# Turning half of each later image's x on VectorE instead of TensorE in a two-layer attention kernel

## The chip, the cores and the metric

The kernel runs on one core of a Trainium2 chip. The metric is the device time of one execution in microseconds. All data is fp32. The engines are named as in the profile: PE (TensorE), PEld (its weight loads), DVE (VectorE), ACT (ScalarE), POOL (GpSimd), SP (SyncE, which here only issues transfers).

## The reference

Input x has 8 images of 32x32 tokens with 512 channels. Two layers follow one another. The change lies in the first:

```
x_flat = x.reshape(8, 1024, 512)
# group norm: 32 groups of 16 channels, over all tokens of an image
mu, var = mean and variance over (tokens, the 16 channels of a group)
x_norm = (x - mu) * rsqrt(var + 1e-6) * gn_scale + gn_bias
q, k, v = split(x_norm @ w_qkv + b_qkv, 3)          # 8 heads of 64
out = softmax(q k^T / 64 per head) @ v               # 1024 queries, 1024 keys
x = x_flat + out @ w_out + b_out
```

(1/64 is the product of the two scalings of q and of k by 1/sqrt(64).) The second layer takes a layer norm of that result, a projection, a 7x7 depthwise convolution of stride 2, from which sampling points come, bilinear samples as keys and values, an attention of 1024 queries over 256 keys, an output projection, and an MLP with residual. Of it only the convolution matters here, since a large part of it is computed during the first layer.

## The kernel before, in words

The first pass handles layer 0. For each image it needs x with the channels on the partitions: xT, two blocks of [128, 4, 512] (partition, chunk c, token), where channel = c*128 + partition. Tokens come in 8 tiles of 128 (`x`, two buffers). `load_x` fetches a tile with 128 partitions of 2 KB, issued by POOL. `turn(t)` transposes it with four PE transposes (moving operand the identity, weights the 128x128 piece of x), copies the PSUM tile to xT by ACT, and issues the load of the tile two later. `two_tiles(i)` runs four bn_stats of 256 tokens on DVE; `gather`, `means`, `deviations`, `factors` make the group statistics with a small matrix `gmat` that averages over the partitions of a group, and `norm(blk)` scales xT in place (ACT for images after the first).

The main loop goes over images b (called blocks here, 0 to 7), four head pairs and 8 query tiles: 32 units per block, 256 in all. The step `att.push` of a unit issues:

1. scores: 16 matmuls into two PSUM tiles `sc` (one for each head of the pair, two buffers in all, so the next unit writes the same two);
2. on DVE the maximum `nmax` of each, on ACT the exponential `e` of each;
3. everything that is due before unit + 0.8 (`before`);
4. on DVE two transposes `sq` of 128x1024; after each second unit 16 transfers by SP turn `sq` into `et`, which the `av` matmuls of two to four units later read;
5. everything that is due before unit + 1 (`after`).

All other work is put on places in units by hand: `at(place, step)`, and `run_due` issues what is due in order of place. A place 8.4 is thus in unit 8 after its scores and exponentials, and 8.9 is after its DVE transposes. `InOrder` keeps every engine's instructions in this program order, and each engine works through its own queue strictly in it. The places that the prediction names:

- `norm_steps` for the next image: turns of tiles 0 to 7 at 8.4, 8.45, 16.4, 16.45, 22.4, 22.45, 23.4, 23.45; statistics at 9.85, 17.86, 22.86, 23.95; the group statistics at 23.97 to 25.81, the scaling at 25.85 and 26.85. Image 0 has the same list before the loop.
- `qkv_steps`, `value_steps`: one projection of 16 or 32 matmuls in most units.
- `out_steps` (blocks 1 to 7, for the image before): `fetch` and `add` (POOL, tile `xr`), `out` (PE), `summed` (DVE: `xr`, `stats`, `mv`, then a power on POOL), `norm` (DVE `hat`, then two products of 128x512 on POOL); `norm` of the rows stands at 4.85, 6.85, 7.85, 8.85, 12.85, 14.85, 15.85, 16.85.
- `conv_chunk` (blocks 2 to 7 in units 1 to 24, blocks 1 to 7 from unit 26): the 49 taps of 128 channels. Most are made by ACT (`part_x`, two buffers, named `oa` for the first) and added to `oa` by POOL; the rest by DVE (`od`). In a unit half of ACT's taps stand at .05 and on, the other half at .9 and on, DVE's at .86 and on. So the late taps of a unit lie in ACT's queue ahead of the next unit's exponentials.

The steps that the change touches:

Of the kernel before, what the change touches and what calls it, by code (L numbers as in the profile page):

```python
# [9 lines left out]
F32 = mybir.dt.float32  # L10
I32 = mybir.dt.int32
AF = mybir.ActivationFunctionType
ALU = mybir.AluOpType
AX = mybir.AxisListType
# [3 lines left out]
P = 128  # L18
# [3 lines left out]
C = 512  # L22
NC = C // P
NT = S // P
QB = 512
NQB = S // QB
NQT = QB // P
# [3 lines left out]
GRP = 16  # L31
# [3 lines left out]
SQ = 32  # L35
NSQ = P // SQ
# [205 lines left out]
def attention_then_deformable_attention(  # L242
# [30 lines left out]
    nc = tc.nc  # L273
    x_tok = x.rearrange("b h w c -> b (h w) c")
# [8 lines left out]
    ident = const.tile([P, P], F32, tag="ident", name="ident")  # L283
# [7 lines left out]
    def mm_tile():  # L291
        return ps_mm.tile([P, QB], F32, tag="mm", name="mm")

    def by_chunk(w):
        return w.rearrange("(c p) o -> p c o", p=P)
# [6 lines left out]
    def load_cols(pool, v, name):  # L302
        t = pool.tile([P, v.shape[0] // P], F32, tag=name, name=name)
        with nc.allow_non_contiguous_dma(reason="a vector onto partitions"):
            nc.sync.dma_start(t, v.rearrange("(c p) -> p c", p=P))
        return t

    def load_row(pool, v, name):
        t = pool.tile([P, C], F32, tag=name, name=name)
        nc.sync.dma_start(t, v.partition_broadcast(P))  # L310
        return t
# [32 lines left out]
    def rstd(dst, var, eps):  # L344
        nc.vector.tensor_scalar(dst, var, eps, None, ALU.add)
        nc.gpsimd.tensor_tensor(dst, dst, minus_half[:, 0 : dst.shape[1]], ALU.pow)
# [15 lines left out]
    def at(place, step):  # L362
        due.append((place, len(due), step))
# [37 lines left out]
    with ExitStack() as l0:  # L401
        wp = l0.enter_context(tc.tile_pool(name="w0", bufs=1))
        work = l0.enter_context(tc.tile_pool(name="work0", bufs=2))

        nc = InOrder(tc)
        NX = 2
        NX_T = 3
        xs = {}

        def load_x(b, t):  # L410
            if b < B:
                xs[b, t] = work.tile([P, C], F32, tag="x", name="x", bufs=NX)
                nc.gpsimd.dma_start(xs[b, t], x_tok[b][ts(t, P), :])


        x2 = work.tile([P, NC, QB], F32, tag="xT", name="x2", bufs=NX_T)
# [3 lines left out]
            xs[0, NQT + t] = x2[:, t, :]  # L420
            nc.sync.dma_start(xs[0, NQT + t], x_tok[0][ts(NQT + t, P), :])
        wqkv = wp.tile([P, NC, 3 * C], F32, tag="wqkv", name="wqkv")
        gsc = load_cols(wp, gn_scale, "gsc")
        gbi = load_cols(wp, gn_bias, "gbi")
        bqkv = load_cols(wp, b_qkv, "bqkv")
        for i in (1, 0, 2):
            nc.sync.dma_start(wqkv[:, :, ts(i, C)], by_chunk(w_qkv)[:, :, ts(i, C)])
        bout = load_row(wp, b_out, "bout")
        room_w = {}

        def load_weight(w):
# [7 lines left out]

        gmat = wp.tile([P, P], F32, tag="gmat", name="gmat")  # L440
        nc.gpsimd.memset(gmat, 1.0 / GRP)
        g3 = gmat.rearrange("p (g c) -> p g c", c=GRP)
        ng = P // GRP
        nc.gpsimd.affine_select(
            out=g3, in_=g3, pattern=[[-GRP, ng], [0, GRP]], compare_op=ALU.is_ge,
            fill=0.0, base=0, channel_multiplier=1,
        )
        nc.gpsimd.affine_select(
            out=g3, in_=g3, pattern=[[GRP, ng], [0, GRP]], compare_op=ALU.is_ge,
            fill=0.0, base=GRP - 1, channel_multiplier=-1,  # L450
        )
        att = MovedAttention(nc, ident, ps_mm, ps_sc, ps_av, work, dram, 1)
        xTs, qkv, vals = {}, {}, {}

        def norm_steps(b, start, places):

            room = {}

            def turn(t):
                blk, i = divmod(t, NQT)  # L460
                if i == 0:
                    xTs[b, blk] = work.tile([P, NC, QB], F32, tag="xT", name="xT", bufs=NX_T)
                if t == 0:
                    room["stats"] = work.tile([P, NC, NT // 2, 6], F32, tag="stats", name="stats", bufs=1)
                ps = mm_tile()
                for c in range(NC):
                    nc.tensor.transpose(ps[:, ts(c, P)], xs[b, t][:, ts(c, P)], ident)
                nc.scalar.copy(xTs[b, blk][:, :, ts(i, P)], ps.rearrange("p (c q) -> p c q", q=P))
                if b > 0:
                    load_x(b + (t + NX) // NT, (t + NX) % NT)  # L470
                elif t < NX:
                    load_x(1, t)

            def two_tiles(i):
                blk, half = divmod(i, NQT // 2)
                for c in range(NC):
                    nc.vector.bn_stats(
                        room["stats"][:, c, i, :], xTs[b, blk][:, c, ts(half, 2 * P)]
                    )


            def gather():
                mv = room["mv"] = work.tile([P, NC, 2], F32, tag="mv", name="mv")
                stats = room["stats"]
                for c in range(NC):
                    nc.vector.bn_aggr(mv[:, c, :], stats[:, c, :, :].rearrange("p s f -> p (s f)"))

            def means():
                mv = room["mv"]
                ps = mm_tile()  # L490
                for m in range(2):
                    half = ds(m * HD, HD)
                    nc.tensor.matmul(
                        ps[half, 0:NC], lhsT=gmat[:, half], rhs=mv[:, :, 0], start=True, stop=True
                    )
                mu = room["mu"] = work.tile([P, NC], F32, tag="mu", name="mu")
                nc.vector.tensor_copy(mu, ps[:, 0:NC])
                dev = room["dev"] = work.tile([P, NC], F32, tag="dev", name="dev")
                nc.vector.tensor_tensor(dev, mv[:, :, 0], mu, ALU.subtract)
                nc.vector.tensor_tensor(dev, dev, dev, ALU.mult)  # L500
                nc.vector.tensor_tensor(dev, dev, mv[:, :, 1], ALU.add)

            def deviations():
                ps = mm_tile()
                for m in range(2):
                    half = ds(m * HD, HD)
                    nc.tensor.matmul(
                        ps[half, 0:NC], lhsT=gmat[:, half], rhs=room["dev"], start=True, stop=True
                    )
                room["rs"] = work.tile([P, NC], F32, tag="rs", name="rs")  # L510
                rstd(room["rs"], ps[:, 0:NC], 1e-6)

            def factors():
                nc.vector.tensor_tensor(room["rs"], room["rs"], gsc, ALU.mult)
                room["add"] = work.tile([P, NC], F32, tag="nadd", name="nadd")
                nc.vector.tensor_tensor(room["add"], room["mu"], room["rs"], ALU.mult)
                nc.vector.tensor_tensor(room["add"], gbi, room["add"], ALU.subtract)

            def norm(blk):
                xT, add, rs = xTs[b, blk], room["add"], room["rs"]  # L520
                for c in range(NC):
                    if b == 0:
                        nc.vector.tensor_scalar(
                            xT[:, c, :], xT[:, c, :], rs[:, c : c + 1], add[:, c : c + 1],
                            ALU.mult, ALU.add,
                        )
                    else:
                        nc.scalar.activation(
                            xT[:, c, :], xT[:, c, :], AF.Identity,
                            bias=add[:, c : c + 1], scale=rs[:, c : c + 1],  # L530
                        )

            steps = [
                *(lambda t=t: turn(t) for t in range(NT)),
                *(lambda i=i: two_tiles(i) for i in range(NT // 2)),
                gather, means, deviations, factors,
                *(lambda blk=blk: norm(blk) for blk in range(NQB)),
            ]
            for place, what in zip(places, steps):
                at(start + place, what)  # L540
# [150 lines left out]
        def conv_chunk(b, cb, n):  # L691
# [79 lines left out]
        first_values = (1.3, 2.3, 3.3, 4.3)  # L771
        value_places = [(-1.7, 2.3, 3.6, 4.3), (10.3, 18.3, 19.3, 20.3)]
        norm_places = [
            *(8.4, 8.45, 16.4, 16.45, 22.4, 22.45, 23.4, 23.45),
            *(9.85, 17.86, 22.86, 23.95),
            *(23.97, 24.03, 25.03, 25.81, 25.85, 26.85),
        ]
        out_places = [3.3, 5.3, 6.3, 7.3, 11.3, 13.3, 14.3, 15.3]
# [10 lines left out]
        for b in range(B):  # L789
# [22 lines left out]
            for hp in range(NHP):  # L812
                for qt in range(NT):
                    n = first + hp * NT + qt
                    if n % per == 0 and b > 0:
# [6 lines left out]
                    t = qkv[b, hp]  # L822
# [5 lines left out]
                        q=t["q", qt // NQT][:, ts(qt % NQT, P)],  # L828
# [8 lines left out]
    with ExitStack() as l1:  # L837
        nc = tc.nc


        def pool(name, bufs=1):
            return l1.enter_context(tc.tile_pool(name=name, bufs=bufs, reuse_waits="tile"))

        first, raw, late, late2, cv, cvhat, wp = (
            pool(n) for n in ("first", "raw", "late", "late2", "cv", "cvhat", "w2")
        )
        work = pool("work1", 2)
        nc = InOrder(tc)
# [89 lines left out]
        chat, room = {}, {}  # L938
# [385 lines left out]
```

## Time and profile before

| what | value |
|---|---|
| median of 3 runs | 3404.53 us (3399.92 to 3406.07) |
| the profiled execution's own time | 3397.38 us |
| its span, first to last instruction | 3395.7 us |
| granted PE clock, mean | 0.99 |
| PE, DVE, ACT, POOL busy | 97%, 73%, 53%, 46% |
| first pass (scores of unit 0 to the last of its work) | 35.8 to 2042 us |
| turns `mm<-ident,x` on PE | 256 instructions, 37.0 us busy |
| `xT<-mm` copies on ACT | 64, mean 588 ns |
| `x<-in_x_dram` issues on POOL | 60, mean 558 ns |

A row of a group gives line, engine, operation, output<-inputs, shape and count, then busy time and mean duration of one in ns, then the engine's idle time just before it and who ended it. A row of a timeline gives start and duration in us, the engine, the operation, how many in a row, and in brackets the idle time before with its releaser. Nearly all instructions are recorded under line 54, the helper that issues them, so rows are told apart by their tiles.

### The profile page before, as it was taken

How to read it: one execution, taken by the hardware profiler on the slowest of the kernel's cores; microseconds unless marked ns; L12 is line 12 of the kernel's file. 1: busy time of each engine (PE TensorE's matmuls, PEld its weight loads, DVE VectorE, ACT ScalarE, POOL GpSimd, SP SyncE). 2: the span in 40 equal slices, each digit the busy share in tenths (PEclk: the TensorE clock that was granted, in tenths of full speed). 3: DMA queues.
4: the chain of work that ended last, by engine and by line, in shares of the span. 5: the costliest groups of instructions: out<-in, count | busy, mean ns of one | idle time of the engine just before them, and what ended most of it. 6: DMA issues, size and time to landing. Idle time of an engine off the chain costs nothing. (4 is left out here: it accounts for less than half of the span.)

```text
span 3395.7 us, 59693 instructions
## 1 busy us (share of the span) xinstructions
PE 3298.7 (97%) x21736; PEld 1348.9 (40%) x21736; DVE 2480.5 (73%) x3373; ACT 1811.4 (53%) x3927; POOL 1547.6 (46%) x1903
## 2 busy tenths in 40 slices
PE   7999999999999999999999998889999999999998
PEld 3344444444344444344344343433333333333332
DVE  5776788888888888888898885157767586664654
ACT  3443365576576566566567561245565555554442
POOL 1002226656746746755755763215455354631322
PEclk9999999999999999999999999899999999999999
DMA  5666766766766766776767667446566565665653
GB/s 153 177 179 164 210 179 196 215 176 183 228 181 184 218 187 180 210 202 179 216 185 187 202 191 205 138 159 200 185 203 197 183 203 185 208 214 191 215 177 126
DMA packets 446645, 642.57 MB, mean 189 GB/s; under 512 B 77104, under 2 KB 240944, under 8 KB 444304
## 3 DMA queue, kind: packets, MB, share of 16 engines
q1 hardware_dynamic: 415712, 536.67, 54.5%
q0 software_dynamic: 29488, 100.00, 9.6%
q8 instruction: 172, 2.82, 0.3%
q10 hardware_dynamic: 1152, 2.10, 0.2%
q14 instruction: 121, 0.99, 0.1%
HBM read 246.38 MB, written 123.73 MB: 109 GB/s over the span
## 5 line engine op out<-in xcount | busy, mean ns | idle before, releaser
L54 ACT ACTIVATE e<-sc,nmax 128x1024 f32<-128x1024 f32 (+1 forms) x1024 | 803.4, 798 | 490.7 <-DVE nmax L54 487.9
L54 DVE TENSOR_REDUCE nmax<-sc 128x1 f32<-128x1024 f32 (+1 forms) x640 | 751.7, 1215 | 337.0 <-PE sc L54 333.0
L54 POOL TENSOR_TENSOR oa<-part_x,oa 128x256 f32<-128x256 f32 x852 | 640.7, 752 | 552.6 <-ACT part_x L54 506.3
L54 DVE STREAM_TRANSPOSE sq<-e 128x1024 f32<-128x1024 f32 x640 | 766.2, 1228 | 156.6 <-ACT e L54 125.1
L54 ACT ACTIVATE part_x<-pad_x,dww_x 128x256 f32<-128x256 f32 x852 | 442.3, 547 | 251.8 <-POOL oa L54 250.7
L54 PE MATMUL sc<-k,q 64*64 64x512 f32 x4096 | 516.6, 602 | 13.5 <-ACT e L54 10.3
L54 PE MATMUL av<-et,v 128*64 128x256 f32 x4096 | 502.5, 388 | 14.1 <-DMA et<-sq 12.5
L54 PE MATMUL mm<-xT,wqkv 128*64 128x512 f32 x2048 | 463.1, 594 | 3.2 <-issue 3.2
L54 PEld LDWEIGHTS av<-et,v 128*64 128x64 f32 x4096 | 275.4, 137 | 332.0 <-issue 170.3
L54 POOL TENSOR_TENSOR chunk<-parts,chunk 128x256 f32<-128x256 f32 x240 | 186.8, 778 | 277.3 <-ACT parts L54 263.4
L54 POOL TENSOR_TENSOR mv<-mv,minus_half 128x1 f32<-128x1 f32 x128 | 76.5, 598 | 510.3 <-DVE mv L54 509.8
L54 PEld LDWEIGHTS sc<-k,q 64*64 64x64 f32 x4096 | 139.2, 132 | 322.1 <-issue 204.0
L54 PEld LDWEIGHTS mm<-xT,wqkv 128*64 128x64 f32 x2048 | 148.3, 138 | 255.0 <-issue 239.6
L54 DVE SCALAR_TENSOR_TENSOR od<-pad_x,dww_x,od 128x256 f32<-128x256 f32 x276 | 232.2, 841 | 5.5
L54 PE MATMUL mm<-wo,attH 128*64 128x512 f32 x1024 | 234.8, 598 | 0.7 <-DVE attH L54 0.7
L54 PE MATMUL mm<-w,attT 128*64 128x512 f32 x1024 | 231.5, 596 | 2.0 <-DVE attT L54 2.0
L54 PE MATMUL mm<-wqkv,xT 128*64 128x256 f32 x2048 | 232.1, 379 | 0.0
L54 PE MATMUL mm<-wm,zT 128*64 128x512 f32 x1024 | 230.7, 592 | 1.0 <-ACT zT L54 1.0
L54 PE MATMUL mm<-hat_h,wqq 128*64 128x512 f32 x1024 | 230.8, 593 | 0.0
L54 ACT ACTIVATION_READ_ACCUMULATOR e<-sc,nmax 128x1 f32 x1024 | 209.3, 204 | 0.0
L54 ACT ACTIVATE parts<-pad,dww 128x256 f32<-128x256 f32 x240 | 126.4, 552 | 124.8 <-POOL chunk L54 124.4
L54 PEld LDWEIGHTS mm<-wqkv,xT 128*64 128x64 f32 x2048 | 148.1, 137 | 77.6 <-issue 6.4
(164 smaller groups left out, 3390.9 us busy)
## 6 DMA issues: line engine op xcount, KB each, us to landing
et<-sq SPq DMA_DIRECT2D x2048, 128.0 KB
sq_d<-sq SPq DMA_DIRECT2D x128, 512.0 KB
et<-sq_d SPq DMA_DIRECT2D x128, 512.0 KB
inv<-rs_d SPq DMA_DIRECT2D x256, 128.0 KB
hat_h<-hat_d SPq DMA_DIRECT2D x16, 1024.0 KB
xr<-mid SPq DMA_DIRECT2D x64, 256.0 KB
x<-in_x_dram POOLq DMA_DIRECT2D x60, 256.0 KB
out_dram<-res POOLq DMA_DIRECT2D x60, 256.0 KB
```

What stands on the lines that cost most here:

```text
L54: return self.tc.keep_in_program_order(op(*args, **kwargs))
```

## The change

Channels are laid out in fours per partition: channel = partition*4 + c. The weights wqkv and the vectors gsc and gbi are loaded accordingly, a group of 16 channels now lies on 4 partitions, so `gmat` has blocks of 4, and the sums over the four columns of a group are made by two small reductions, with one value per partition for mean and deviation.

For images after the first, tiles 0 to 3 are loaded by four transfers, one for each quarter of the channels: quarter r goes to partitions 32r to 32r+31, partition 32r+q holding that quarter (128 channels, 512 bytes) of the tokens 4q to 4q+3. One DVE transpose in blocks of 32x32, which reads and writes with a step of 4 elements, then makes the tile of xT directly in SBUF. Tiles 4 to 7, and all of image 0, are turned by PE as before, but read x with a step of 4 elements. The loads leave `turn` and become steps `more(t)` of their own. New places: turns at 1.9, 4.9, 7.9, 10.9 for tiles 0 to 3; loads at 4.2 (tile 2), 7.2 (tile 3), 10.2 and 12.5 (tiles 4, 5), 22.46 and 22.47 (tiles 6, 7), 26.4 and 27.2 (tiles 0 and 1 of the image after); the second statistics step at 15.86 instead of 17.86.

```diff
@@ load_x
-                nc.gpsimd.dma_start(xs[b, t], x_tok[b][ts(t, P), :])
+                src, dst = x_tok[b][ts(t, P), :], xs[b, t]
+                if b > 0 and t < NQT:
+                    src = src.rearrange("(q t) (r x) -> r q t x", t=NSQ, r=NSQ)
+                    dst = dst.rearrange("p (t x) -> p t x", t=NSQ)
+                    for r in range(NSQ):
+                        nc.gpsimd.dma_start(dst[ts(r, SQ)], src[r])
+                    return
+                nc.gpsimd.dma_start(dst, src)
...
-        gsc = load_cols(wp, gn_scale, "gsc")
-        gbi = load_cols(wp, gn_bias, "gbi")
+        gsc, gbi = (wp.tile([P, NC], F32, tag=n, name=n) for n in ("gsc", "gbi"))
+        for tile_, v in ((gsc, gn_scale), (gbi, gn_bias)):
+            nc.sync.dma_start(tile_, v.rearrange("(p c) -> p c", p=P))
...
-            nc.sync.dma_start(wqkv[:, :, ts(i, C)], by_chunk(w_qkv)[:, :, ts(i, C)])
+            nc.sync.dma_start(
+                wqkv[:, :, ts(i, C)], w_qkv.rearrange("(p c) o -> p c o", p=P)[:, :, ts(i, C)]
+            )
...
@@ turn
-                ps = mm_tile()
-                for c in range(NC):
-                    nc.tensor.transpose(ps[:, ts(c, P)], xs[b, t][:, ts(c, P)], ident)
-                nc.scalar.copy(xTs[b, blk][:, :, ts(i, P)], ps.rearrange("p (c q) -> p c q", q=P))
+                to = xTs[b, blk][:, :, ts(i, P)]
+                if b > 0 and blk == 0:
+                    nc.vector.transpose(
+                        to.rearrange("p c (q t) -> p t c q", t=NSQ),
+                        xs[b, t].rearrange("p (t i c) -> p t c i", t=NSQ, i=SQ),
+                    )
+                else:
+                    ps = mm_tile()
+                    by_row = xs[b, t].rearrange("p (i c) -> p c i", c=NC)
+                    for c in range(NC):
+                        nc.tensor.transpose(ps[:, ts(c, P)], by_row[:, c], ident)
+                    nc.scalar.copy(to, ps.rearrange("p (c q) -> p c q", q=P))
+                if b == 0 and t < NX:
+                    load_x(1, t)
+
+            def more(t):
                 if b > 0:
                     load_x(b + (t + NX) // NT, (t + NX) % NT)
-                elif t < NX:
-                    load_x(1, t)
...
@@ means, deviations, factors
-                nc.vector.tensor_copy(mu, ps[:, 0:NC])
+                nc.vector.tensor_reduce(mu, ps[:, 0:NC], AX.X, ALU.add)
...
-                rstd(room["rs"], ps[:, 0:NC], 1e-6)
+                one = room["one"] = work.tile([P, 1], F32, tag="one", name="one")
+                nc.vector.tensor_reduce(one, ps[:, 0:NC], AX.X, ALU.add)
+                rstd(one, one, 1e-6)
...
             steps = [
                 *(lambda t=t: turn(t) for t in range(NT)),
+                *(lambda t=t: more(t) for t in range(NT)),
...
@@ norm_places
-            *(8.4, 8.45, 16.4, 16.45, 22.4, 22.45, 23.4, 23.45),
-            *(9.85, 17.86, 22.86, 23.95),
+            *(1.9, 4.9, 7.9, 10.9, 22.4, 22.45, 23.4, 23.45),
+            *(4.2, 7.2, 10.2, 12.5, 22.46, 22.47, 26.4, 27.2),
+            *(9.85, 15.86, 22.86, 23.95),
```

More of the change, by code (lines that the diff above doesn't have):

```diff
@@ L441, in attention_then_deformable_attention @@
         nc.gpsimd.memset(gmat, 1.0 / GRP)
-        g3 = gmat.rearrange("p (g c) -> p g c", c=GRP)
-        ng = P // GRP
+        rows = GRP // NC
+        g3 = gmat.rearrange("p (g c) -> p g c", c=rows)
+        ng = P // rows
         nc.gpsimd.affine_select(
-            out=g3, in_=g3, pattern=[[-GRP, ng], [0, GRP]], compare_op=ALU.is_ge,
+            out=g3, in_=g3, pattern=[[-rows, ng], [0, rows]], compare_op=ALU.is_ge,
             fill=0.0, base=0, channel_multiplier=1,
@@ L448, in attention_then_deformable_attention @@
         nc.gpsimd.affine_select(
-            out=g3, in_=g3, pattern=[[GRP, ng], [0, GRP]], compare_op=ALU.is_ge,
-            fill=0.0, base=GRP - 1, channel_multiplier=-1,
+            out=g3, in_=g3, pattern=[[rows, ng], [0, rows]], compare_op=ALU.is_ge,
+            fill=0.0, base=rows - 1, channel_multiplier=-1,
         )
@@ L495, in means @@
                     )
-                mu = room["mu"] = work.tile([P, NC], F32, tag="mu", name="mu")
-                nc.vector.tensor_copy(mu, ps[:, 0:NC])
+                mu = room["mu"] = work.tile([P, 1], F32, tag="mu", name="mu")
+                nc.vector.tensor_reduce(mu, ps[:, 0:NC], AX.X, ALU.add)
                 dev = room["dev"] = work.tile([P, NC], F32, tag="dev", name="dev")
-                nc.vector.tensor_tensor(dev, mv[:, :, 0], mu, ALU.subtract)
+                nc.vector.tensor_scalar(dev, mv[:, :, 0], mu, None, ALU.subtract)
                 nc.vector.tensor_tensor(dev, dev, dev, ALU.mult)
@@ L509, in deviations, with factors @@
                     )
+                one = room["one"] = work.tile([P, 1], F32, tag="one", name="one")
+                nc.vector.tensor_reduce(one, ps[:, 0:NC], AX.X, ALU.add)
+                rstd(one, one, 1e-6)
+            def factors():
                 room["rs"] = work.tile([P, NC], F32, tag="rs", name="rs")
-                rstd(room["rs"], ps[:, 0:NC], 1e-6)
-            def factors():
-                nc.vector.tensor_tensor(room["rs"], room["rs"], gsc, ALU.mult)
+                nc.vector.tensor_scalar(room["rs"], gsc, room["one"], None, ALU.mult)
                 room["add"] = work.tile([P, NC], F32, tag="nadd", name="nadd")
-                nc.vector.tensor_tensor(room["add"], room["mu"], room["rs"], ALU.mult)
+                nc.vector.tensor_scalar(room["add"], room["rs"], room["mu"], None, ALU.mult)
                 nc.vector.tensor_tensor(room["add"], gbi, room["add"], ALU.subtract)
```

## The prediction

> **What bounds the kernel now.** I read the page first, then the busy time of the first pass as one stretch, then timelines of single units by engine. PE is busy 97% of the span, and in the first pass (35.8 to 2042 us) 1991.51 of 2006.20 us at full clock.
>
> ```profile
> PE 3298.7 (97%) x21736; PEld 1348.9 (40%) x21736; DVE 2480.5 (73%) x3373; ACT 1811.4 (53%) x3927; POOL 1547.6 (46%) x1903
> ...
> 35.80:2042.00 2006.20, 1991.51 (x13964) 837.59 (x13966) 1662.76 (x2015) 1179.32 (x2180) 1012.54 (x1275) 1.00 0.69 190
> ```
>
> Columns of the second line: stretch, length, busy us of PE, PEld, DVE, ACT, POOL, clock, DMA share, GB/s. So a unit lasts as long as its matmuls: from one score burst to the next 7.2 us with one projection, 10.6 with two. What the change removes stands here, in PE's timeline (start, duration) of block 4, unit 16:
>
> ```profile
> 1175.79 2.06 PE L54 MATMUL sc<-k,q 64*64 64x512 f32 x16
> ...
> 1179.58 3.60 PE L54 MATMUL mm<-xT,wqkv 128*64 128x512 f32 x16
> 1183.11 1.09 PE L54 MATMUL mm<-ident,x 128*128 128x128 f32 x8
> 1184.13 1.95 PE L54 MATMUL sc<-k,q 64*64 64x512 f32 x16
> ```
>
> Two turned tiles hold the next scores back by 1184.13 - 1183.11 = 1.02 us.
>
> But PE leads by little. A second ring runs through every unit: scores, maximum (DVE), exponentials (ACT), and only then may the next scores overwrite the PSUM tiles. In units with convolution taps ACT's queue has a tap's product ahead of the exponentials, and that waits for POOL to free one of two part buffers. POOL's timeline of block 4, unit 5, then ACT's, then PE's:
>
> ```profile
> 1077.43 2.42 POOL L54 TENSOR_TENSOR oa<-part_x,oa 128x256 f32<-128x256 f32 x3 [3.37 <-ACT part_x L54]
> 1079.81 1.46 POOL L54 TENSOR_TENSOR xr<-xr,bout 128x512 f32<-128x512 f32 x1
> ...
> 1083.17 1.34 POOL L54 TENSOR_TENSOR hat<-hat,lnb_row 128x512 f32<-128x512 f32 x1
> 1084.47 2.35 POOL L54 TENSOR_TENSOR oa<-part_x,oa 128x256 f32<-128x256 f32 x3
> ```
>
> ```profile
> 1085.23 0.57 ACT L54 ACTIVATE part_x<-pad_x,dww_x 128x256 f32<-128x256 f32 x1 [4.80 <-POOL oa L54]
> 1085.70 1.10 ACT L54 ACTIVATE e<-sc,nmax 128x1024 f32<-128x1024 f32 x1
> ...
> 1086.80 1.10 ACT L54 ACTIVATE e<-sc,nmax 128x1024 f32<-128x1024 f32 x1
> ```
>
> ```profile
> 1089.08 1.95 PE L54 MATMUL sc<-k,q 64*64 64x512 f32 x16
> ```
>
> The second exponential ends at 1087.9, 1.2 us before the scores that need its PSUM tile. POOL is 1.2 us from being the bound. In unit 13 the reserve is nil (ACT, then PE):
>
> ```profile
> 1155.65 1.10 ACT L54 ACTIVATE e<-sc,nmax 128x1024 f32<-128x1024 f32 x1
> ...
> 1156.74 1.10 ACT L54 ACTIVATE e<-sc,nmax 128x1024 f32<-128x1024 f32 x1
> ```
>
> ```profile
> 1157.93 2.00 PE L54 MATMUL sc<-k,q 64*64 64x512 f32 x16
> ```
>
> It ends at 1157.84, 0.1 us ahead of PE, and again behind a tap that waited for POOL. In unit 16 it is DVE that is late:
>
> ```profile
> 1179.87 2.35 DVE L54 TENSOR_REDUCE nmax<-sc 128x1 f32<-128x1024 f32 x2
> ```
>
> The scores of that unit were there at 1175.79 + 2.0; the maximum starts 2.1 us later because DVE was still busy. Its second exponential (1182.25 for 1.12) ends 0.8 us before unit 17's scores, and that only because the two turns stand between.
>
> **What is removed.** Tiles 0 to 3 of images 1 to 7: 28 tiles, 14 pairs at units 8.4 and 16.4. PE: 14 x 1.02 = 14.3 us. The pair of block 0, unit 8 lies in a unit with no projection, where the scores wait for the exponentials anyway (units 8 and 9 together last 12.89 us there, an empty unit and the next 4.58 + 8.31 = 12.89), so 13.3 us count. ACT loses 28 copies of 0.59 us, POOL two loads (1.13 us) at each of 8.4 and 16.4.
>
> **What is added.** Three items.
>
> (a) DVE, 28 transposes of 128x512. The nearest row is the transpose of 128x1024 at 1228 ns, and 128x32 at 212: a fixed 0.18 and 1.02 ns an element, so 0.70 us. New is that both sides step by 16 bytes. The reads of ACT from PSUM at that step cost nothing (k 684 ns, the plain q 683), so I take 0.70; the upper end is twice the element time, 1.24; below 0.61, half the large one, nothing points. They stand in the order after taps at units 1, 4, 7 and 10.
>
> (b) POOL: 28 loads become 112, since each of four quarters is an issue of its own: 84 more at 0.54 to 0.58 us, as the pair at 1115.51 took 1.13. Four issues are 2.25 us, standing at 4.2 and 7.2 and, for the next image, 26.4 and 27.2; single ones at 10.2 and 12.5.
>
> (c) The statistics of the second half of block 0 of xT, four instructions in 1.38 us, move from 17.86 to 15.86.
>
> Small ones: two extra reductions per image, on 128x4 (0.15 us each), against a power on 128x1 instead of 128x4 (598 against 1042 ns): about -0.3 us once at the start, where it is on the path, hidden in the later blocks by unit 24 and 25's slack on DVE; if it weren't hidden, below 2 us in all. gsc, gbi and wqkv move the same bytes in a like number of instructions on SP, and gsc is not wanted before 20.5 us: nothing. The smaller packets of x (512 bytes) hide in 25 us between load and turn, with the DMA engines at 0.69; uncovered it would be a few us in one block.
>
> **Where PE then waits,** by blocks. Block 0 has neither taps nor output rows: -1.0. Block 1 has no taps at these units: unit 8 gives 1.0; in unit 16 the maximum comes 1.38 late with 2.2 us of reserve, less the 1.02 that goes: 0.2 lost. So -1.8. Blocks 2 to 6 have everything:
>
> Unit 5: the four issues at 4.2 stand behind `oa` x3 and before `xr`, where POOL has no gap until the exponentials: +2.25. The reserve was 1.2 us, so PE waits 2.25 - 1.2 + 0.1 = +1.15. DVE's own turn at 4.9 is covered by that.
> Unit 8: -1.02. The turn at 7.9 puts the maximum 0.7 later against 2.3 of reserve less 1.02; the issues at 7.2 find 0.8 us of gap and get 1.13 back at 8.4. Nothing more.
> Units 10 to 13: the turn at 10.9 has no gap after it (DVE is busy through unit 12): +0.7, with 0.2 brought from unit 9, so the exponentials of 12 come 0.9 later, the taps follow them, and the issue at 12.5 adds 0.57: unit 13's come 1.47 later, without reserve: PE +1.4.
> Units 14 to 17: DVE, POOL and ACT hand that on; unit 15 had no reserve either. In unit 16 the moved statistics stand ahead of the maximum: 1.47 + 1.38 = 2.85 later, so the exponentials end at 1183.4 + 2.85 = 1186.2 where the next scores had stood at 1184.13. At unit 17 PE is 2.0 us behind, not 1.02 ahead. Unit 17, with two projections, takes up the rest.
>
> Per block 1.15 - 1.02 + 2.0 = +2.1; five blocks +10.6. The sum: 10.6 - 1.0 - 1.8 - 0.3 = +7.5 us. On the profiled execution's own 3397.4 (span 3395.7) that gives 3404.9; that execution lies 7.1 below the median of the three runs, 3404.5, so I give 3412.0.
>
> [...] Of 36 tiles still turned on PE the weight loads now step by 16 bytes. The trace has a step of 8 on this side, and it costs nothing:
>
> ```profile
> L54 PEld LDWEIGHTS mm<-wvv,smp 128*64 128x64 f32 x256 | 20.7, 138 | 32.5 <-issue 30.5
> L54 PEld LDWEIGHTS mm<-ident,x 128*128 128x128 f32 x256 | 29.2, 147 | 31.3 <-issue 25.5 <-ACT part_x L54 4.1 <-DMA x<-in_x_dram 0.9
> ```
>
> [...] By the row the sum has 0. [...]
>
> **Rivals.** First, the side engines absorb it: the taps on DVE take 0.45 to 0.84 us depending on what POOL does, and issues leave DVE free, so the delays may not add up. With unit 5's loss alone: -13.3 + 5.8 = -7.5, 3397; with none, and the present waits of units 14 and 16 (0.1 to 0.4 each) gone too, -15, 3390. Against it speak the reserves of 0.1 and 1.2 us above. It decides below about 0.8 us lost per block. 20%.
> Second, strided reads are slow: +12 to +27, 3417 to 3432. It decides where the x turns' weight loads exceed 200 ns. 17%.
> Third, nothing moves: the tiles turned earlier wait for loads instead and the gain and loss are each about nil: 3404. With loads 25 us ahead this is 3%.
> The forecast, 60%: +0.5 to +15, 3405 to 3420, its lower end if units 12 to 16 pass on half.
>
> **Numbers.** About 0.2%, 6.8 us, is what this kernel's measurement tells from no change. Of the forecast's 60 points 37 lie above 3411.3 and 23 within; the first rival puts 16 below 3397.7 and 4 within; the second 17 above, of the third all within. With a little moved from the crowded edge: faster 0.16, same 0.29, slower 0.55. The range 3396 to 3430 leaves out the best of the first rival and the worst of the second.
>
> **What would show it.** `mm<-ident,x` 256 to 144 and `x<-in_x_dram` on POOL 60 to 144. In blocks 2 to 6, unit 5 at 11.8 us instead of 10.6, unit 8 at 7.2, unit 13 near 12, unit 16 about 8.9; PE's waits for `ACT e` in the first pass grow from 3 to some 15 us. It is wrong if unit 16 falls to 7.2 and unit 5 stays at 10.6, or if the weight loads of x leave 147 ns or the new DVE row leaves 0.7 us.

## The result and the profile after

The changed kernel takes 3430.65 us, median of 5 runs (3425.98 to 3436.87), against 3404.53 us for the kernel before in the same comparison (3399.92 to 3407.58): ratio 1.0084, 95% interval 1.0069 to 1.0100. It is about 26 us slower. The profiled execution took 3430.65 us, with a span of 3428.6 us at a mean granted clock of 0.988 (before: 3395.7 us, 0.99). The traced difference of 32.9 us is larger than 26 because the profiled execution before lay 7 us under its median.

First the busy times of the page, then the first pass as one stretch (length; busy us of PE, PEld, DVE, ACT, POOL; clock; DMA share; GB/s):

```profile
PE 3314.7 (97%) x21624; PEld 1344.5 (39%) x21624; DVE 2492.6 (73%) x3409; ACT 1797.2 (52%) x3899; POOL 1592.6 (46%) x1987
...
35.50:2074.00 2038.50, 2007.09 (x13846) 832.98 (x13848) 1681.12 (x2049) 1165.13 (x2151) 1051.35 (x1352) 1.00 0.68 187
```

PE has 112 matmuls fewer, as intended, and yet 15.6 us more busy time in the first pass. The score matmuls alone (tile `sc`) grow from 503.66 to 528.95 us there at an equal count of 4016. One record of a score matmul lasts 0.59 to 0.64 us, so a wait of that order between two of them leaves no gap, and a burst that waits in its middle is recorded as busy. The new operations on the tile `x` (minimum/median/maximum in ns, first and last start):

```profile
L54 POOL DMA_DIRECT2D x<-in_x_dram x144: 538/552/707, 1.4 to 1783.9; - x144
L54 PEld LDWEIGHTS mm<-ident,x x144: 195/210/230, 5.5 to 1791.5; 128*128 128x128 f32 x144
...
L54 DVE STREAM_TRANSPOSE xT<-x x28: 1105/1152/1185, 48.0 to 1684.6; 128x512 f32<-128x512 f32 x28
```

The counts are as predicted. The turn on DVE takes 1152 ns, not 700, and the weight loads of x 210 ns (141 before).

The place of the loss is read from the distance of one score burst to the next. The table, worked out from the traces, gives the mean over blocks 2 to 6 for every unit that moved by more than 0.1 us from before to after, here with the experiments told of below (us):

| kernel | 5 | 6 | 8 | 9 | 12 | 13 | 14 | 16 | 17 | 22, 23 |
|---|---|---|---|---|---|---|---|---|---|---|
| before | 10.62 | 10.62 | 8.21 | 10.62 | 7.35 | 10.62 | 10.80 | 8.41 | 10.62 | 8.21 |
| after | 10.90 | 11.94 | 7.19 | 12.15 | 8.30 | 11.35 | 11.71 | 7.98 | 11.74 | 8.35 |
| e1 no step | 10.90 | 11.91 | 7.19 | 12.15 | 7.86 | 11.38 | 11.71 | 7.99 | 11.74 | 8.35 |
| e2 one issue | 10.62 | 11.30 | 7.19 | 10.97 | 8.52 | 11.14 | 11.70 | 7.98 | 11.75 | 8.35 |
| e3 both | 10.62 | 10.88 | 7.19 | 11.20 | 8.66 | 10.84 | 11.46 | 7.96 | 11.75 | 8.35 |
| e4 statistics back | 10.90 | 11.60 | 7.19 | 12.10 | 8.29 | 11.37 | 11.71 | 7.42 | 11.02 | 8.35 |
| e5 wq first | 10.90 | 11.60 | 7.19 | 10.97 | 8.68 | 11.06 | 11.66 | 7.99 | 11.74 | 8.35 |
| e6 layout | 10.62 | 10.62 | 8.35 | 10.62 | 7.40 | 10.62 | 10.87 | 8.55 | 10.62 | 8.35 |
| e7 places | 10.62 | 10.62 | 7.19 | 10.62 | 8.38 | 10.62 | 10.81 | 7.37 | 10.86 | 8.35 |

The stall that the prediction put into unit 5 shows at the burst after it, so its length falls to unit 6. POOL, ACT and PE in block 4 after:

```profile
1086.78 1.62 POOL L54 TENSOR_TENSOR oa<-part_x,oa 128x256 f32<-128x256 f32 x2
1088.35 2.23 POOL L54 DMA_DIRECT2D x<-in_x_dram  x4
1090.59 1.29 POOL L54 TENSOR_TENSOR xr<-xr,bout 128x512 f32<-128x512 f32 x1
```

```profile
1095.78 0.56 ACT L54 ACTIVATE part_x<-pad_x,dww_x 128x256 f32<-128x256 f32 x1 [6.82 <-POOL oa L54]
1096.24 1.10 ACT L54 ACTIVATE e<-sc,nmax 128x1024 f32<-128x1024 f32 x1
...
1097.33 1.11 ACT L54 ACTIVATE e<-sc,nmax 128x1024 f32<-128x1024 f32 x1
```

```profile
1097.60 2.91 PE L54 MATMUL sc<-k,q 64*64 64x512 f32 x16
```

The tap product waited 6.82 us for POOL where it had waited 4.80. The second exponential ends at 1098.4, after the burst has begun, so the burst takes 2.91 us instead of 1.95: the wait is inside it and no list of waits shows it in full. DVE is not late here. Its timeline of this unit before, then after:

```profile
1079.18 4.20 DVE L54 SCALAR_TENSOR_TENSOR od<-pad_x,dww_x,od 128x256 f32<-128x256 f32 x3
1083.30 2.34 DVE L54 TENSOR_REDUCE nmax<-sc 128x1 f32<-128x1024 f32 x2
```

```profile
1087.73 1.99 DVE L54 SCALAR_TENSOR_TENSOR od<-pad_x,dww_x,od 128x256 f32<-128x256 f32 x3
1089.77 1.18 DVE L54 STREAM_TRANSPOSE xT<-x 128x512 f32<-128x512 f32 x1
1090.82 2.33 DVE L54 TENSOR_REDUCE nmax<-sc 128x1 f32<-128x1024 f32 x2
```

Two of DVE's three taps now run beside the four issues and not beside products of POOL, and the three take 1.99 us instead of 4.20. Even with the turn in between, the maximum starts 3.8 us after the unit's first score; before, it was 4.8.

The largest new loss was not in the prediction at all. The four issues of the second tile at 7.2 are followed on POOL by the issue of the next weights (`load_weight(wq)` at 7.6), and a projection that stands between the scores of units 9 and 10 needs them (POOL before, POOL after, then PE and PE's waits in the first pass after; columns us in total, times, longest):

```profile
1107.35 0.81 POOL L54 DMA_DIRECT2D w<-in_L_conv_wq_dram  x1
```

```profile
1117.16 2.26 POOL L54 DMA_DIRECT2D x<-in_x_dram  x4
1119.41 0.80 POOL L54 DMA_DIRECT2D w<-in_L_conv_wq_dram  x1
```

```profile
1128.31 7.09 PE L54 MATMUL mm<-w,hat_x 128*64 128x512 f32 x32 [0.71 <-DMA w<-in_L_conv_wq_dram]
```

```profile
PE mm L54 <- DMA w<-in_L_conv_wq_dram: 5.4, 5, 1.7
PE sc L54 <- ACT e L54: 5.4, 8, 1.3
```

The first of these waits does not stand among those of before. Counted from the first score of unit 8, the issue stood at 0.5 us before and stands at 2.7 to 3.1 us after, and these weights land some 7.8 us after an issue (median of 13 in the trace after). At the same time the two turns that are gone let the projection come 1.02 us sooner: it began 11.87 us after that score before, and begins at 10.84 where nothing waits (e7 below).

The last two places, first DVE in unit 11 of block 4, before and after:

```profile
1133.22 2.31 DVE L54 SCALAR_TENSOR_TENSOR od<-pad_x,dww_x,od 128x256 f32<-128x256 f32 x2
1135.46 2.34 DVE L54 TENSOR_REDUCE nmax<-sc 128x1 f32<-128x1024 f32 x2
```

```profile
1142.82 3.40 DVE L54 SCALAR_TENSOR_TENSOR od<-pad_x,dww_x,od 128x256 f32<-128x256 f32 x2
1146.14 1.15 DVE L54 STREAM_TRANSPOSE xT<-x 128x512 f32<-128x512 f32 x1
1147.18 2.31 DVE L54 TENSOR_REDUCE nmax<-sc 128x1 f32<-128x1024 f32 x2
```

The maximum comes 2.1 us later after the unit's first score (2.5 before, 4.65 after), and only half of that is the turn. The other half is the second tap: 1.38 us before, 2.45 after, in each of blocks 2 to 6. POOL after, at that moment:

```profile
1143.38 0.56 POOL L54 DMA_DIRECT2D x<-in_x_dram  x1
1143.96 1.28 POOL L54 TENSOR_TENSOR xr<-xr,bout 128x512 f32<-128x512 f32 x1
```

The load at 10.2 now stands ahead of the product `xr`, which therefore starts just after the tap does (1143.76) and not before it, and three products of taps follow without a gap. DVE in unit 16:

```profile
1192.32 1.40 DVE L54 BATCH_NORM_STATS2 stats<-xT 128x6 f32<-128x256 f32 x4
1193.63 2.34 DVE L54 TENSOR_REDUCE nmax<-sc 128x1 f32<-128x1024 f32 x2
```

In both units the moved work stands directly ahead of the maximum with no idle time of DVE before the reduction.

### The profile page after: what moved, and what is told of

Same layout as the page of the kernel before. It is cut to its first block, busy times and chain, and to the rows that moved or that the text cites. A ratio compares the mean times of both kernels' runs of the same rounds, so it can differ in the third digit from the quotient of the medians.

```text
span 3428.6 us, 59616 instructions
## 1 busy us (share of the span) xinstructions
PE 3314.7 (97%) x21624; PEld 1344.5 (39%) x21624; DVE 2492.6 (73%) x3409; ACT 1797.2 (52%) x3899; POOL 1592.6 (46%) x1987
## 3 DMA queue, kind: packets, MB, share of 16 engines
q10 hardware_dynamic: 1152, 2.10, 0.2%
## 4 chain that ended last, share of the span: by engine, by line
PE 69%; POOL 8%; DMA 7%; ACT 6%; DVE 5%; issue 3%; SPq 3%; POOLq 0%; ACTq 0%; DVEq 0%
PE mm L54 44%; PE sc L54 13%; PE av L54 12%; ACT e L54 4%; SPq L54 3%; POOL oa L54 2%; POOL hat L54 1%; DVE nmax L54 1%; DMA w<-in_L_conv_wq_dram 1%; DMA row<-mid,ii 1%; POOL xr L54 1%; DMA sq_d<-sq 1%; DVE sq L54 1%; POOL chunk L54 1%; DMA et<-sq_d 1%
## 5 line engine op out<-in xcount | busy, mean ns | idle before, releaser
L54 PE MATMUL sc<-k,q 64*64 64x512 f32 x4096 | 542.3, 604 | 18.4 <-ACT e L54 14.5
L54 DVE SCALAR_TENSOR_TENSOR od<-pad_x,dww_x,od 128x256 f32<-128x256 f32 x276 | 219.7, 796 | 5.5
L54 POOL DMA_DIRECT2D x<-in_x_dram x144 | 80.0, 560 | 214.3 <-PE mm L54 123.3
```

Of the source, the lines that this page charges most:

```text
L54: return self.tc.keep_in_program_order(op(*args, **kwargs))
```

## The experiments

Theory A: the stepped transpose is the main loss. Theory B: POOL's four issues for each tile, and what is queued behind them. Theory C: the statistics at 15.86. Each ratio is to the kernel before as measured at the same time; the medians of before lie between 3398.9 and 3405.1 us.

**e1, no step in DVE's turn.**

```diff
-                        to.rearrange("p c (q t) -> p t c q", t=NSQ),
-                        xs[b, t].rearrange("p (t i c) -> p t c i", t=NSQ, i=SQ),
+                        to.rearrange("p c (t q) -> p t c q", t=NSQ),
+                        xs[b, t].rearrange("p (t c i) -> p t c i", t=NSQ, i=SQ),
```

> Changed kernel, but VectorE's turn reads and writes without a step of four elements; the values of those 28 tiles are thereby arranged in another order than the computation wants, instructions and bytes are the same. Theory A (the stepped transpose is the main loss: 28 turns at 1152 ns instead of about 0.70 us, all in the path): 28 x 0.45 = 12.6 us back, about 3418 us. Theory B (POOL's four issues per tile and what stands behind them are the main loss): only the turns in unit 12 of blocks 1 to 6 are in the path, 6 x 0.45 = 3 us back, about 3428 us; unit 6 and unit 9 keep their +1.0 and +1.1 to +1.9 us. Theory C (the earlier statistics): as B, unit 17 keeps its +1.1 us.

```profile
L54 DVE STREAM_TRANSPOSE xT<-x x28: 669/698/712, 48.1 to 1684.2; 128x512 f32<-128x512 f32 x28
```

Measured: ratio 1.0062 (1.0041 to 1.0084), median 3429.8 us against 3405.1. In blocks 2 to 6 only unit 12 gets shorter, by 0.44 us on average: 2.2 us in five blocks. The 0.45 us saved per turn comes back in one place of four. The expectation of theory A, about 3418 us, lies just outside the interval (3419 to 3434 us), and the trace agrees: theory A falls.

**e2, one issue for each tile.** The branch with four `dma_start` in `load_x` is taken out.

> Changed kernel, but each x tile is loaded by one DMA instead of four by quarters (x issues 144 to 60); the values of the 28 turned tiles are in another arrangement than the computation wants, all else is the same. Theory A: the turns stay, so at most 2 to 3 us back, about 3428 us. Theory B: unit 6 loses its +1.0 us (the four issues at 4.2 no longer delay oa's three instructions), unit 9 its +1.1 to +1.9 us (the wq load at 7.6 stands behind one issue), unit 12 or 14 some 0.5 us (the taps beside the issues at 12.5): about 3 us in each of six blocks, 15 to 18 us back, 3412 to 3416 us, and PE no longer waits for the DMA of w from conv_wq. Theory C: nothing, 3430 us.

PE's waits in the first pass of this run:

```profile
PE sc L54 <- ACT e L54: 5.5, 9, 0.8
PE av L54 <- DMA et<-sq: 3.8, 2, 3.2
```

Measured: ratio 1.0025 (1.0011 to 1.0038), median 3416.7 against 3405.1 us: more than half of the loss is gone, near theory B's figure. The wait for the weights has gone, and unit 9 falls from 12.15 to 10.97; 0.35 us over before remain there. Unit 6, from which theory B expected 1.0 us, gives back only 0.64 us on average, and 0.28 in each of blocks 2, 3, 4 and 6. The reason is on DVE, in block 4 of this run:

```profile
1086.26 6.00 DVE L54 SCALAR_TENSOR_TENSOR od<-pad_x,dww_x,od 128x256 f32<-128x256 f32 x3
1092.18 1.16 DVE L54 STREAM_TRANSPOSE xT<-x 128x512 f32<-128x512 f32 x1
1093.23 2.31 DVE L54 TENSOR_REDUCE nmax<-sc 128x1 f32<-128x1024 f32 x2
```

This delay was not there in the changed kernel; the edit makes it. The same three taps took 4.20 us before and 1.99 beside four issues, and with a single issue ahead of POOL's products they take 6.00: one tap of the three lasts 3.6 us. With the turn, the maximum starts 7.7 us after the unit's first score instead of 4.8 before.

**e3, both edits.**

> Both edits at once: VectorE's turn without a step, and one DMA per x tile (values of the 28 turned tiles arranged in another order than the computation wants). If A and B are independent the gains add: B's 15 to 18 and 3 us, about 3410 us; then what is left over the kernel before (3404.5) is the stepped PE loads (some 2 us) and the moved statistics (unit 17). If both hide behind the same wait, it is no better than the better of the two alone. Theory C: about 3425 us.

Measured: ratio 1.0028 (1.0017 to 1.0039), median 3414.6 against 3405.1 us; not separable from e2. In the trace unit 6 falls further, to 10.88, where now the shorter turn counts. The wait for the weights is back in three of the five blocks (1.7 us in all), although only one issue stands ahead of theirs: unit 9 has 11.20 here and 10.97 in e2. Some 9 us remain over the kernel before; units 17, 22 and 23 have kept theirs, and units 12 to 14 together 2.2 of their 2.6 us.

**e4, statistics back at 17.86.** One number in `norm_places`.

> Changed kernel with the second statistics step back at place 17.86, nothing else; correct computation. Theory C (the statistics at 15.86 are what lengthens unit 17 by 1.1 us): unit 17 back, unit 16 back to its old length (+0.5): about 0.7 us in each of six blocks, 4 us, about 3426 us. Theories A and B: the 1.4 us of statistics lies in the path at either place, so no change within 2 us, 3430 us; unit 17 would then keep its +1.1 because the burst's phase comes from units 12 to 14.

DVE at unit 16 of block 4, with no statistics before the maximum:

```profile
1195.79 0.55 DVE L54 TENSOR_SCALAR hat<-xr,mv 128x512 f32<-128x512 f32 x1
1196.24 2.35 DVE L54 TENSOR_REDUCE nmax<-sc 128x1 f32<-128x1024 f32 x2
```

Measured: ratio 1.0046 (1.0028 to 1.0063), median 3423.1 us. Units 16 and 17 together fall from 19.72 to 18.44: 1.28 us a block, almost the whole 1.40 us of the four instructions, and 6.4 us in five blocks. The mechanism of theory C holds, with more than the 4 us expected of it, and it is independent of B: units 9 and 12 to 14 have not moved. The two ratios lie 0.38% apart, about 13 us; what came on top of the 6.4 is not explained by these units.

**e5, second tile's load behind the weights' load** (7.65 instead of 7.2).

> Changed kernel with the second tile's load at place 7.65 instead of 7.2, so that its four issues stand on POOL behind the one of conv_wq (7.6) and not ahead of it; correct computation. Theory B, its second half (the matmul of wq waits for its weights because their issue stands behind four x issues): unit 9 returns from 11.8-12.5 us to 10.6-11.0, 1.1 to 1.9 us in each of blocks 2 to 6, 5 to 8 us back, 3423 to 3425 us, and PE no longer waits for the DMA of w from conv_wq. If the wait only hid another one in unit 9 (the exponential of unit 8's burst), unit 9 stays within 0.5 us and the time at 3430 us.

Measured: unit 9 falls from 12.15 to 10.97, just as in e2, so the order on POOL alone makes 1.18 of the 1.53 us, and the wait for the weights is gone from PE's list. What makes the other 0.35, in e2 as here, was not traced. The ratio, 1.0068 (1.0043 to 1.0093), median 3425.7 against 3402.2 us, agrees with the expected 5 to 8 us but its interval overlaps that of the changed kernel; the trace carries this verdict, not the time. Units 12 and 13 together kept theirs.

**e6, the layout alone.** Everything turned on PE with its step of four, single loads, all places as before.

> Layout alone: channels in fours per partition, but all tiles turned by TensorE at the places of before (8.4, 8.45, 16.4, ...), one load per tile after its turn, statistics at their places of before; correct computation. TensorE then loads all 288 pieces of x at 210 ns instead of 137. Measured already: a pair of tiles costs 1.16 us instead of 1.02 in the turn's unit. 29 pairs x 0.14 = 4.1 us more than before and 2 us in the start: 3408 to 3411 us. If the layout cost nothing, 3404.5; if it were the main loss, 3425 or more.

Measured: ratio 1.0016 (1.0003 to 1.0030), median 3408.5 against 3402.2 us. Units 8, 16, 22 and 23 are longer by 0.14 us each, none of the others in these blocks by more than 0.07. The layout costs what the longer weight loads cost (210 ns in the changed kernel, 141 before): four units in seven or eight blocks, about 4 us, of which the changed kernel (two of these units, and the turns of image 0) keeps about half.

**e7, other places.**

```diff
-            *(1.9, 4.9, 7.9, 10.9, 22.4, 22.45, 23.4, 23.45),
-            *(4.2, 7.2, 10.2, 12.5, 22.46, 22.47, 26.4, 27.2),
-            *(9.85, 15.86, 22.86, 23.95),
+            *(0.81, 0.82, 3.9, 3.91, 22.4, 22.45, 23.4, 23.45),
+            *(1.0, 2.0, 9.96, 9.97, 22.46, 22.47, 26.4, 27.2),
+            *(6.95, 9.85, 22.86, 23.95),
```

> Changed kernel, same instructions, other places: turns at 0.81, 0.82, 3.9 and 3.91 (VectorE stood idle 2.5 to 2.9 us ahead of a reduction there), loads at 1.0, 2.0, 9.96 and 9.97 (POOL idle), statistics at 6.95 and 9.85 instead of 9.85 and 15.86; correct computation. If places are what was lost (theories B and C): units 8 and 16 keep their -1.02 us each in six blocks (-12 us), unit 17 loses 1.1 us more, units 6, 9 and 12 to 14 are as before, PE's stepped loads cost 2 us: about 3393 to 3398 us, faster than before. If the stepped transposes cost wherever they stand (theory A, 28 x 1.15 = 32 us of VectorE in a kernel without slack): 3415 us or more.

DVE in unit 3 of block 4, then PE's longest wait in the first pass:

```profile
1070.52 2.16 DVE L54 STREAM_TRANSPOSE xT<-x 128x512 f32<-128x512 f32 x2
1073.33 2.36 DVE L54 TENSOR_REDUCE nmax<-sc 128x1 f32<-128x1024 f32 x2 [0.65 <-PE sc L54]
```

```profile
PE av L54 <- DMA et<-sq: 11.2, 4, 3.5
```

Measured: ratio 0.9995 (0.9983 to 1.0007), median 3400.1 against 3402.2 us: the whole loss is gone with the same instructions at other places of turns, loads and statistics. The tap in unit 11 is back at 1.38 us. Two stepped turns in a row still leave DVE idle 0.65 us before the maximum. But there is no gain either. Units 8 and 16 keep their 1.02 us, and units 5, 6, 9, 13 and 14 are as before; unit 17 keeps 0.24 us; unit 12 now lasts 10.41 and 9.93 us in two of five blocks and 7.19 in the others. There `av` waits for the transfers of `et`. The expected 3393 to 3398 us were not reached.

**e8, 128-byte runs.** Before's layout and weights; only the four tiles are loaded by quarters that lie scattered (runs of 32 channels), with e7's places.

```diff
+                    src = src.rearrange("(q t) (c r i) -> r q t c i", t=NSQ, r=NSQ, i=SQ)
+                    dst = dst.rearrange("p (t c i) -> p t c i", t=NSQ, i=SQ)
```

> Kernel before with its own order of channels (no change to weights, gains, means; TensorE reads without a step), but the first four tiles of images 1 to 7 loaded by quarters in runs of 128 bytes and turned by VectorE, which reads without a step and writes with a step of four; places of turns, loads and statistics as in the run of other places; correct computation. TensorE's loads of x back at 137 ns: 2 us better than the run of other places in units 22 and 23, and 2 us in the start; the turn between 0.70 and 1.15 us. Against it: 512 packets of 128 bytes an issue instead of 128 of 512 bytes: POOL's issues longer than 0.56 us. If they take 4 times as long (2.2 us, 9 us a tile), POOL's products (oa, part_x) come late and the time is 3430 us or more; if they stay near 0.56 us, 3390 to 3396 us.

```profile
L54 POOL DMA_DIRECT2D x<-in_x_dram x144: 538/652/711, 1.4 to 1757.6; - x144
L54 PEld LDWEIGHTS mm<-ident,x x144: 138/141/231, 6.4 to 1765.0; 128*128 128x128 f32 x144
...
L54 DVE STREAM_TRANSPOSE xT<-x x28: 1064/1108/1141, 41.7 to 1593.1; 128x512 f32<-128x512 f32 x28
```

Measured: ratio 1.0001 (0.9986 to 1.0016), median 3397.8 against 3402.2 us: not separable from the kernel before. An issue that describes four times as many runs takes 0.65 us, not 2.2. The weight loads are back at 141 ns and units 22 and 23 at 8.21. The wait in unit 12 stays, here in block 6:

```profile
1659.97 1.95 PE L54 MATMUL sc<-k,q 64*64 64x512 f32 x16
1665.86 3.68 PE L54 MATMUL av<-et,v 128*64 128x256 f32 x16 [3.94 <-DMA et<-sq]
```

**e9 and e10, one side of the turn stepped** (one execution each; the halves of e1's diff).

> Changed kernel with VectorE's turn reading with a step of four and writing without one (values of the 28 turned tiles arranged in another order than the computation wants): a price for the reading side alone. Both sides stepped took 1152 ns, none 698 ns. If the read side carries it: 1.1 us; if the write side does: 0.70 us; if the two add: about 0.92 us. In the run of 128-byte loads, where only the write side was stepped, it took 1108 ns, so 0.70 to 0.75 us is expected.

> Changed kernel with VectorE's turn writing with a step of four and reading without one (values of the 28 turned tiles arranged in another order than the computation wants): expected 1.1 us by the run of 128-byte loads, if it is the write side that carries the price, whatever the layout around it.

The turn with a stepped read, then with a stepped write:

```profile
L54 DVE STREAM_TRANSPOSE xT<-x x28: 1064/1126/1149, 48.9 to 1684.9; 128x512 f32<-128x512 f32 x28
```

```profile
L54 DVE STREAM_TRANSPOSE xT<-x x28: 1065/1124/1148, 48.7 to 1684.3; 128x512 f32<-128x512 f32 x28
```

The first came out at the figure named for a read side that carries the price, and not at the 0.70 to 0.75 us expected; the second came out as expected. So neither side carries it alone: either of them costs nearly all of it (698 to about 1125 ns), and with both sides stepped it takes 1152 ns at the same places and 1122 at those of e7. Their single times, 3424.1 and 3421.0 us, say nothing more.

**e11, e8 with two stores of `hat` on POOL instead of SP, and e12, the kernel before with the same.**

```diff
-                to_hat.dma_start(hat_d[b][:, t, :], hat)
+                (nc.gpsimd if t in (2, 3) else to_hat).dma_start(hat_d[b][:, t, :], hat)
```

> The kernel with loads of 128-byte runs, and the stores of hat for tiles 2 and 3 of the image before issued by POOL instead of SP (two issues of 0.4 to 0.6 us with their gaps leave SP between units 8 and 9); correct computation. Theory S (the 1.02 us saved in unit 8 are given back in unit 12, where the product waits for the transfers of et that SP issues one after the other, so SP's queue is the next limit): unit 12 back to 7.2 us in most of blocks 1 to 7, and 4 to 10 us less than with the stores on SP: 3388 to 3394 us. Rival (the waits of unit 12 come from the landing of the transfers, not from SP's issues): unit 12 keeps 9 to 14 us in two to four blocks, 3398 us; or POOL's later products cost what SP gains.

> Control: the kernel before with the same two stores of hat on POOL; correct computation. Theory S: in it unit 12 hardly waits, so nothing is to be gained: 3401 to 3406 us, within 0.1% of the kernel before. If it gains as much as the run beside it, the gain there has nothing to do with the change.

Measured: e11 has ratio 0.9982 (0.9971 to 0.9993), median 3392.3 against 3398.9 us; e12 0.9992 (0.9984 to 1.0001). So e11 is the one version whose interval lies wholly below the kernel before, by 2 to 10 us. But theory S is not shown. PE's waits for `et` in the trace of e11:

```profile
PE av L54 <- DMA et<-sq: 10.5, 5, 3.8
```

e8 had 9.9 us of them. Unit 12 lasts 12.75 us in block 6 and 9.25 in block 1, though five of the seven blocks are now under 8 us. The intervals of e8 and e11 overlap, and part of the gain may be the control's. Whether the waits of unit 12 come from SP's issues or from the landing of the transfers stays open.

## Why the prediction was wrong

The direction was right and the size was not: +7.5 us predicted, about 26 measured, just outside the range. Two steps of the sum failed. "Nothing more" for the four issues at 7.2 left out the issue of weights behind them on POOL (7.7 us). And the sum for units 10 to 14 took the turn too short and held the durations of DVE's taps fixed while it moved POOL's work about (6 us more than predicted). Against its terms, in blocks 2 to 6:

- **Unit 5: +1.15 predicted, +0.97 found** in blocks 2, 3, 4 and 6, as the burst of unit 6. POOL's delay was right. That the turn at 4.9 adds nothing was right too, but not because it is covered: the issues made DVE's taps shorter by 2.2 us, more than the turn takes. Block 5 lost 3.2 us more in units 5 and 6: 1.4 us of it stayed in e1, e4 and e5 and went with the four issues (e2, e3); there POOL stands still for 1.55 us between the first and the second issue, for a reason that the profile does not show. The other 1.6 us were absent in e4 and e5 and are taken for scatter.
- **Unit 8: -1.02, found exactly.**
- **Unit 9: "Nothing more" predicted for the issues at 7.2, 1.1 to 1.9 us found.** This is the step that failed most. POOL's gap was counted for the products behind it, but the next instruction there was the issue of weights, whose landing PE awaits one unit later; and the 1.02 us saved in unit 8 let PE need them that much sooner. On average unit 9 is longer by 1.5 us in each of five blocks, 7.7 us; e2 and e5 both remove 1.2 of the 1.5.
- **Units 10 to 14: +1.4 predicted, +2.6 found** (28.77 to 31.36 for units 12 to 14). The turn was taken at 0.70 us instead of 1.15, which explains 0.4 (e1). The single load at 10.2 was put at nothing: with it there, the tap ahead of the turn takes 2.45 us instead of 1.38. That tap takes 2.4 to 2.5 us in blocks 2 to 6 of all eight kernels traced with the load at 10.2 (after, e1 to e5, e9, e10) and 1.4 in all six without it. Turn, tap and the issue at 12.5 (0.54) together make 2.8 us, about what was found; that they add up in this way is an estimate, since no run moved the load at 10.2 alone.
- **Units 16 and 17: about +0.6 predicted beyond that, +0.69 found.** e4 shows the statistics as the cause, at 1.28 us a block.
- **Units 22 and 23: 0 predicted, +0.27 found**, from the longer weight loads, as in e6.

The sum of these is 5.0 us a block instead of 2.1, or 25 instead of 10.6 in five blocks; with block 5's own 3.2 it is 28. Block 0 gave -1.4 (predicted -1.0). Block 1 gave +0.1 instead of -1.8: units 8 and 16 gave their two microseconds, and unit 12 took 1.4 back. Block 7, without any of the change's turns, lost 6.3 in the trace, of which 5.1 in unit 12; e6, with no turn on DVE, has 6.6 there and e1 none, so it needs none of the turns; it is taken for scatter, which one trace of each kernel cannot show. Adding the blocks of the trace gives 33 us, of which 7 is the profiled execution's distance from its median.

The prediction's own signs of being wrong came: the weight loads left 147 ns and the turn left 0.7 us. The row of the 8-byte step (138 ns) was no measure for 16 bytes: there a weight load takes 210 ns instead of 141, and the turn on DVE 1152 instead of 698. That strided reads would be slow was an estimate of the second rival, and at this step it was right; its size was not. Its +27 us, which the chances and the range take up, has 20 us for weight loads twice as long, nearly all in PE's path, and no run shows that term: a load grew by half, eight of them by 0.55 us together, and a pair of tiles costs 0.14 us more (e6), so about 4 us with all tiles on PE and half of that in the changed kernel. For DVE the upper end of 1.24 us was near.

The second rival had the decisive point right (loads over 200 ns) and the cause wrong: strides account for the 0.27 us a block of PE and some 0.4 in unit 12, about 4 us of the 26. Its 3417 to 3432 us hold the measured time by luck. The first rival's reason, that taps depend on what POOL does and that issues leave DVE free, is borne out in unit 5 (three taps in 1.99 us beside issues, 4.20 beside products), and turns against it in unit 11 (one tap 2.45 instead of 1.38); its 0.84 us is a mean, and single taps of the kernel before already last up to 2.35 us. Its end, delays absorbed, is what happens when places are chosen anew (e7), and there a wait in unit 12 takes the gain. PE's waits for `ACT e` rose from 3.8 to 5.4 us, not to 15: the stalls fell inside bursts, where they lengthen the burst.

## What to carry to other kernels

When an issue is put into a queue, follow the queue to the next instruction that anyone waits for, not only to the next arithmetic: here the order of one issue of weights and four issues of x made 1.18 us a block in unit 9 (e5). An issue moved in one engine's queue can also change the durations on another: three taps of DVE took 4.20, 1.99 or 6.00 us with no, four or one issue of x ahead of POOL's products, so read every engine again after such a move. And the 27% of DVE's time that was idle did not make moved work free everywhere: the same 28 turns and 112 issues, with the statistics moved too, cost 26 us at one list of places and nothing at another (e7), where DVE still waits 0.65 us for PE behind two turns in a row (unit 3 of block 4).

## What the runs showed of the hardware

A transpose of 128x512 fp32 on DVE in 32x32 blocks takes 698 ns without a step, about 1125 ns with a 16-byte step on either side alone, and 1152 ns with it on both (1122 at the places of e7): here nearly the whole price came with the first stepped side. A weight load of 128x128 fp32 takes 210 ns at a 16-byte step and 141 without. An issue of x on POOL takes 0.54 us for a whole tile, 0.55 for a quarter in runs of 512 bytes and 0.65 for a quarter in four times as many runs of 128 bytes, so what made a tile's loading long here was the number of issues (2.23 us for four). A tap on DVE (128x256) took 0.46 us on average where no product ran on POOL (22 taps of the trace before) and as long as 2.35 us beside products (3.60 in e2); beside issues without products it took 0.48 (14 taps of the trace after).
